# One visit instead of two: where a row tile's attention logits are multiplied in the first propagation step

## The chip, the cores and the metric

The kernel runs on one core of one Trainium2 chip. A core has five engines with queues of their own that meet only through semaphores: TensorE (PE: matrix products and transposes; PEld is its weight load), VectorE (DVE), ScalarE (ACT), GpSimd (POOL) and SyncE (SP, which here only issues DMAs). The metric is the device time of one execution in microseconds (us). Before the change the median of three runs is 1532.81 us (1531.89 to 1533.17).

## The reference, cut to what matters

Two graph layers follow one another on 2708 nodes with 256 features. The change lies in the first of them. It takes two propagation steps; each multiplies by a row-normalised adjacency matrix R, and by an attention matrix A that is computed anew in each step:

```
q = X @ W1.T @ W2.T                        # N x 64
k = X @ W3.T                               # N x 64
logits = q @ k.T                           # N x N
probs = softmax(logits)                    # per row
keep the largest of a row until their sum reaches 0.9, drop the rest, renormalise -> A
Xf = R @ Xf ;  Xa = A @ Xa ;  Z = Z + Xf @ U1[n].T + Xa @ U2[n].T
```

The second layer is a four-headed graph attention, and is not touched.

## The kernel before

**Tiles.** The 2708 rows are cut into 22 row tiles, sixteen of 128 rows and six of 110 (`rows`). For transposing, the tiles go in six groups (`groups`): four of four 128-row tiles, one of four 110-row tiles, one of two.

**What a row tile of step 0 needs.** `scores` (line 780) multiplies a row tile's q with all k. The contraction is 64 long, so the 2708 columns are held as two halves of 1354, one on partitions 0 to 63 and one on 64 to 127, and the two halves of a piece go through the two halves of the PE array. A half is cut into `pieces` of 512, 512 and 330 columns. For each piece the two products go into the two PSUM banks of a tile `lg`, and one ACT instruction takes the exponential of both banks into the row's `e` and sums it into a column of `zp`. POOL adds the three sums to `z` and makes `tau`, 0.9 of it. DVE then finds the row's threshold (`candidates`, `settle`, lines 888 and 899) and writes the kept values over `e` (line 965). After that PE transposes `e` group by group into `tr`, ACT copies each group to `eT`, and PE multiplies it with the features into the accumulator `att` (`turned` and `weigh`, lines 261 and 274); `e` has three buffers, so a tile is searched about three tiles ahead of its use.

**PSUM.** Its eight banks are all given out (line 564): four to `lg` (two buffers of two banks), one each to `walk0` and `walk1`, one to `att`, one to `tr`. In step 0 `free_bank` (line 650) hands out `walk0` and `walk1` in turn to the projections that follow a finished tile: the transposes of `xa` (line 774), a product with the next step's q and k weights for every second tile (line 761), and the term products (line 1252).

**The order.** TensorE, ScalarE, VectorE and GpSimd carry out the order in which the program writes their instructions. `step` (line 1307) takes the tiles in turn, and for each the six groups: first the *next* group's transposes and copy, then this group's products, then a *slot* (line 1292). A slot advances each running search by one stage, may begin a new search, advances the pieces that follow a finished tile, and then one stage of the mixing of adjacency blocks on POOL. Counting slots from 0, the search of tile t + 3 begins in slot 4 of tile t, and its stages stand so: slot 4, logits and exponentials of two pieces; slot 5, the third piece and the sums; slots 0 and 1 of the next tile, the maxima of the candidates; slot 2, the threshold; slot 3, the kept values. Tiles 0, 1 and 2 are searched ahead of the loop, beside the first projections (`terms1`, line 1231); the third of these searches is only half through when the loop begins. The last three tiles of step 0 begin no search.

**A tile boundary on PE.** After the last whole group of tile t PE carries out, in this order: the transposes of the first group of tile t + 1, the two products of tile t's last group, the third logit piece (slot 5), the transposes of the second group of tile t + 1, and the first products of tile t + 1. These last write `att`, which has one buffer: they wait until ACT has read tile t's sum out of it (`xa`, line 1325).

**DMAs.** SP's order is not written out by hand: a scheduler places the DMAs. SP stores the first terms (`c1`, line 1245) from the staging tile `cs`, which has two buffers, and loads the adjacency blocks that POOL mixes (`fetch`, line 677); before the first mixing POOL clears a column of each new block (line 702), and the load waits for that.

Of the kernel before, what the change touches and what calls it, by code (L numbers as in the profile page):

```python
# [8 lines left out]
F32 = mybir.dt.float32  # L9
BF16 = mybir.dt.bfloat16  # L10
I32 = mybir.dt.int32
AF = mybir.ActivationFunctionType
# [4 lines left out]
P = 128  # L17
# [28 lines left out]
def kernel(  # L46
# [16 lines left out]
    nc = tc.nc  # L63
    N, D = x.shape
    DA = w1T.shape[1]
    STEPS = u1T.shape[0]
    H, _, FO = gat_w.shape
# [8 lines left out]
    groups = []  # L76
# [8 lines left out]
    small = ctx.enter_context(tc.tile_pool(name="small", bufs=4))  # L85
# [122 lines left out]
    def share(g, tr):  # L208

        span, m = spans[g], rows[spans[g][0]]  # L210
        k = len(span) * H
        nc.tensor.transpose(
            tr[:k, 0, :m],
            s_src[:m, span[0] : span[-1] + 1, :].rearrange("p t h -> p (t h)"), ident[:m, :m],
        )
        nc.scalar.activation(line[:k, :m], tr[:k, 0, :m], AF.Exp, scale=1.0 - NEG_SLOPE)
        nc.sync.dma_start(shared[g], line[:k, :m])

    def spread(g, r):

        lines = shared[g].rearrange("(t h) m -> h t m", h=H)
        n = len(spans[g]) * rows[spans[g][0]]
        for k in range(2):
            for h in range(2):
                nc.sync.dma_start(
                    r[k][:, h, :n].rearrange("p (t m) -> p t m", t=len(spans[g])),
                    lines[2 * k + h].partition_broadcast(P),
                )
# [25 lines left out]
    def room(pool):  # L254

        return [
            pool.tile([P, N], F32, name="e")[:, : 2 * GW].rearrange("p (h i) -> p h i", h=2)
            for _ in range(2)
        ]
# [292 lines left out]
    def fast_layer0(ep, adjp):  # L552
# [69 lines left out]
        qT = keep.tile([P, N], F32, name="qT")  # L622
# [8 lines left out]
        kT = [wk.tile([P, HN], F32, name="junk"), keep.tile([P, HN], F32, name="kT1")]  # L631
# [15 lines left out]
        walking = []  # L647
        turns_taken = [0]

        def free_bank():  # L650

            if walking:
                return ps_lg.tile([P, 2, CHUNK], F32, name="lg")[:, 0].rearrange(
                    "p (a b) -> p a b", a=4
                )
            turns_taken[0] ^= 1
            return ps_wk.tile([P, CHUNK], F32, name=f"walk{turns_taken[0]}").rearrange(
                "p (a b) -> p a b", a=4
            )
# [120 lines left out]
        def scores(s, t):  # L780

            m = rows[t]
            cols = slice(off[t], off[t + 1])
            e = ep.tile([P, N], F32, name="e")
            halves = e.rearrange("p (h n) -> p h n", h=2)
            zp = small.tile([P, 3], F32, name="zp")
            for n, (c0, w) in enumerate(pieces):
                lg = ps_lg.tile([P, 2, CHUNK], F32, name="lg")
                for h in range(2):
                    part = slice(h * DA, (h + 1) * DA)  # L790
                    nc.tensor.matmul(  # L791
                        lg[:m, h, :w], qT[part, cols], kT[s][part, c0 : c0 + w],
                        start=True, stop=True,
                    )
                nc.scalar.activation(  # L795
                    halves[:m, :, c0 : c0 + w], lg[:m, :, :w], AF.Exp,
                    accum_out=zp[:m, n : n + 1],
                )
                if n == 1:
                    yield  # L800
            z = facts[s][0][:m, t : t + 1]
            nc.gpsimd.tensor_add(z, zp[:m, 0:1], zp[:m, 1:2])
            nc.gpsimd.tensor_add(z, z, zp[:m, 2:3])
            tau = new("tau", m)
            nc.gpsimd.tensor_scalar(tau, z, TOP_P, None, op0=ALU.mult)
            return e, z, tau

        def new(name, m):
            return small.tile([P, 1], F32, name=name)[:m]
# [161 lines left out]
        def search(s, t):  # L971

            e, z, tau = yield from scores(s, t)
            if s:
                seen = yield from survey(t, e, z, tau)
                src, rest = bound(t, e, z, tau, *seen)
            else:
                src, rest = e, tau
            yield
            cand = yield from candidates(s, t, src)  # L980
            yield
            ready[t] = e, (yield from settle(s, t, e, cand, rest))
# [231 lines left out]
        def after_attention0(t, xa):  # L1214

            m = rows[t]
            yield
            if t % 2 == 0:
                pair[:] = [rowp.tile([P, DC, 2 * P], F32, name="xT2", bufs=1)]
            both = pair[0]  # L1220
            xT = both[:, :, m * (t % 2) : m * (t % 2 + 1)]
            tp = free_bank()
            turn(xa, m, tp, nc.scalar.copy, xT)
            yield
            if t % 2:
                pj = free_bank().rearrange("p a b -> p (a b)")
                project(1, off[t - 1], 2 * m, pj, both, nc.scalar.copy, nc.scalar.copy)
                yield
            terms2(t, xT)
# [52 lines left out]
        early, walked, blending, begun, rows_kept = [], [], [], [], []  # L1282
# [4 lines left out]
        def advance(parts):  # L1287
            for g in list(parts):
                if next(g, parts) is parts:
                    parts.remove(g)  # L1290

        def slot(spend, begin=None):

            advance(going)
            if begin and begin[1] < NT:
                going.append(search(*begin))
                next(going[-1])
            advance(doing)
            if begun:
                next(mixing, None)  # L1300
            owed[0] += spend
            while owed[0] > 0:
                owed[0] -= 1
                if next(stream, True):
                    break

        def step(s, cur, spend):
            turned_first = None
            for t in range(NT):
                m = rows[t]  # L1310
                e, rden = ready[t]
                ac = ps_at.tile([P, CHUNK], F32, name="att")
                if s == 0 and t == NT - 1:
                    list(mixing)
                if s and t == NT - 2:
                    share(0, free_bank())
                if s and t == NT - 1:
                    ahead.extend(room(ep))
                    spread(0, ahead)

                def between(n):
                    last = n == len(groups) - 1
                    if last:
                        xa = heldp.tile([P, D], F32, name="xa1")
                        nc.scalar.activation(xa[:m], ac[:m, :D], AF.Copy, scale=rden)  # L1325
                        if s and t in c3:
                            nc.scalar.dma_start(c3[t][:m], xa[:m])
                            stored.add(t)
                        elif s:
                            held[t] = xa  # L1330
                        else:
                            doing.append(after_attention0(t, xa))
                    if (s, t) == (0, NT - 1):
                        for name, at in (("T3", 1), ("T2", 2), ("T1", 2), ("T4", 4)):
                            if n == at:
                                for part in J_PARTS:
                                    blend(name, *part)
                        if last:
                            next(stream)
                    slot(spend[n], (s, t + 3) if n == len(groups) - 2 else None)  # L1340

                def turn_next(n):
                    u = t + n // len(groups)
                    if u == NT:
                        return None
                    return turned(ready[u][0], rows[u], n % len(groups), tpp, ps_tr, nc.scalar.copy)

                turned_first = weigh(
                    ac[:m, :D], turned_first or turn_next(0), m,
                    lambda j: cur[: rows[j], j, 0:D], turn_next, between,  # L1350
                )
                ready.pop(t)
# [43 lines left out]
        with tc.manual_schedule(engines=engines):  # L1396
            query_weights()
            ahead = turn_x(groups[0])
            for n in range(len(groups)):
                c0, w = ahead  # L1400
# [430 lines left out]
```

## Time and profile before

| | |
|---|---|
| median of three runs | 1532.81 us |
| the profiled execution's own time | 1534.79 us |
| its span | 1532.7 us |
| granted TensorE clock over the span | 0.995 |
| busy share of the span: PE, DVE, ACT, POOL | 97%, 83%, 53%, 39% |
| step 0's attention loop | about 72 to 442 us |
| from tile to tile in it, first `att` product to first `att` product | 16.8 us, and 17.7 us in the tiles that also project q and k (128 rows) |
| step 0 loop from 72 to 397 us: PE, DVE, ACT, POOL busy | 323.6, 288.5, 141.9, 193.5 of 325 us |

The span is what the profiler recorded from the first instruction to the last; the execution's own time adds what lies around it. "Busy" counts the time in which an engine has an instruction in work. A busy PE is not yet a PE at its peak, since matmuls are pipelined and their ends are modelled: distances from start to start tell more than durations. In the timeline a row gives start, length, engine, line, operation, tiles, shape and how many instructions were merged (xN); a 32-bit product or transpose stands as one or more passes, and the count is that of passes. Bracketed is the idle time before the row and what ended it.

### The profile page before, as it was taken

To read this page: it belongs to the slowest core of one execution; us is meant where nothing else is said; L and a number is where in the kernel's file an instruction comes from. 1 tells how busy PE (TensorE), PEld (TensorE's weight loads), DVE (VectorE), ACT (ScalarE), POOL (GpSimd) and SP (SyncE) were. 2 spreads that over 40 slices of the span, in tenths; PEclk is the share of its full clock that TensorE was granted. 3 is DMA by queue.
4 is the path that set the end of the run, shared out by engine and by line. 5 is a ranking of instruction groups with operands and counts; after the bars stand their busy time and mean duration, and the time that the engine had idled before them with its cause. 6 is when DMAs were issued, how large, how long until landed. Compare 5 with 4: busy or idle time off the path is not lost. (4 is left out here: it accounts for less than half of the span.)

```text
span 1532.7 us, 29967 instructions
## 1 busy us (share of the span) xinstructions
PE 1492.8 (97%) x10537; PEld 1064.6 (69%) x10537; DVE 1277.1 (83%) x3749; ACT 804.9 (53%) x1495; POOL 594.5 (39%) x959
## 2 busy tenths in 40 slices
PE   8999999999999999999999999999999999999996
PEld 4477777776778889988988888887898223433343
DVE  3699888999714978888889898989895998999996
ACT  3444444444326556655655666666653344456474
POOL 0046657566013323323454554544444310035143
PEclk9999999999999999999999999999999999999998
DMA  6288888878037755554564555555455355334331
GB/s 166 66 246 277 247 247 281 266 234 255 12 102 235 211 165 167 161 162 137 159 199 142 165 183 170 182 166 178 137 151 178 109 172 167 100 104 135 88 105 53
DMA packets 214488, 255.97 MB, mean 167 GB/s; under 512 B 42145, under 2 KB 180541, under 8 KB 214329
## 3 DMA queue, kind: packets, MB, share of 16 engines
q1 hardware_dynamic: 205622, 246.62, 53.7%
q10 hardware_dynamic: 8707, 7.35, 1.5%
q8 instruction: 85, 1.39, 0.4%
q14 instruction: 74, 0.61, 0.1%
HBM read 190.10 MB, written 62.44 MB: 165 GB/s over the span
## 5 line engine op out<-in xcount | busy, mean ns | idle before, releaser
L816 ACT ACTIVATE junk<-e,minus,rth 128x2708 bf16<-128x2708 f32 (+1 forms) x88 | 232.9, 2646 | 52.5 <-POOL rth L848 51.7
L271 ACT COPY eT<-tr 128x512 f32<-128x512 f32 (+5 forms) x264 | 141.5, 536 | 199.0 <-PE tr L266 196.5
L284 PE MATMUL att<-xm,eT 128*128 128x256 f32 (+3 forms) x968 | 230.8, 379 | 0.3 <-ACT xa L1325 0.3
L284 PE MATMUL att<-ba,eT 128*128 128x256 f32 (+3 forms) x968 | 230.9, 379 | 0.0
L1618 PE MATMUL acc<-pt,v 128*32 128x512 f32 (+3 forms) x2112 | 222.9, 543 | 2.1 <-DVE pt L1606 1.1
L1606 DVE SCALAR_TENSOR_TENSOR pt<-e,tj,blk 128x1024 f32<-128x1024 f32 (+3 forms) x176 | 186.6, 1125 | 8.3 <-ACT xw L1265 5.4
L284 PEld LDWEIGHTS att<-xm,eT 128*128 128x128 f32 (+3 forms) x968 | 169.6, 186 | 22.0 <-ACT xa L1325 0.7
L284 PEld LDWEIGHTS att<-ba,eT 128*128 128x128 f32 (+3 forms) x968 | 169.5, 186 | 22.0 <-ACT eT L271 0.8
L795 ACT ACTIVATE e<-lg 128x1024 f32<-128x1024 f32 (+1 forms) x132 | 121.0, 921 | 105.7 <-PE lg L791 102.2
L1109 PE MATMUL walk<-xe,blk 128*128 128x128 f32 (+3 forms) x1386 | 172.9, 275 | 1.2 <-ACT xw L1123 0.7
L1109 PEld LDWEIGHTS walk<-xe,blk 128*128 128x128 f32 (+1 forms) x1386 | 164.4, 187 | 11.4 <-issue 7.4
L1618 PEld LDWEIGHTS acc<-pt,v 128*32 128x32 f32 (+1 forms) x2112 | 73.4, 109 | 130.8 <-issue 76.2
L266 PE MATMUL tr<-ident,e 128*128 128x128 f32 (+3 forms) x968 | 147.5, 271 | 4.8 <-ACT eT L271 4.8
L266 PEld LDWEIGHTS tr<-ident,e 128*128 128x128 f32 (+3 forms) x968 | 111.3, 139 | 47.1 <-issue 26.7
L1109 PE MATMUL walk<-xm,blk 128*128 128x128 f32 (+3 forms) x1034 | 131.3, 277 | 5.4 <-DVE u_sb L1119 2.9
L1109 PEld LDWEIGHTS walk<-xm,blk 128*128 128x128 f32 (+3 forms) x1034 | 124.2, 188 | 14.0 <-issue 6.1
L1628 PE MATMUL acc<-pt,sb 128*32 128x512 f32 (+3 forms) x1056 | 115.7, 542 | 0.0
L1606 DVE SCALAR_TENSOR_TENSOR pt<-r,tj,blk 128x1024 f32<-128x1024 f32 (+1 forms) x88 | 109.9, 1312 | 1.3 <-issue 0.6
L247 ACT ACTIVATE blk<-blk 128x1024 f32<-128x1024 f32 (+3 forms) x66 | 63.3, 960 | 82.5 <-DMA blk<-in_adjT_dram 76.2
L896 DVE MAX8 cand<-e 128x8 f32<-128x170 f32 (+1 forms) x352 | 85.9, 320 | 21.1 <-ACT e L795 21.0
L896 DVE MAX8 cand<-scr 128x8 f32<-128x97 f32 (+1 forms) x616 | 102.8, 244 | 0.0
L914 DVE MAX8 top<-work 128x8 f32<-128x128 f32 (+3 forms) x242 | 82.3, 340 | 8.3
(283 smaller groups left out, 2410.2 us busy)
## 6 DMA issues: line engine op xcount, KB each, us to landing
blk<-in_adjT_dram SPq DMA_DIRECT2D x68, 512.0 KB
blk<-S SPq DMA_DIRECT2D x48, 512.0 KB
blk<-D SPq DMA_DIRECT2D x24, 512.0 KB
blk<-in_adjT_dram SPq DMA_DIRECT2D x26, 440.0 KB
D<-blk SPq DMA_DIRECT2D x16, 512.0 KB
S<-scr SPq DMA_DIRECT2D x16, 512.0 KB
S<-blk SPq DMA_DIRECT2D x16, 512.0 KB
xm<-S SPq DMA_DIRECT2D x16, 512.0 KB
```

The lines of the kernel that those rows point to most:

```text
L247: nc.scalar.activation(bar, bar, AF.Sign)
L266: nc.tensor.transpose(tr[: rows[t], q, :m], e[:m, off[t] : off[t + 1]], ident[:m, :m])
L271: copy(eT[:k, : len(grp), :m], tr[:k, : len(grp), :m])
L284: nc.tensor.matmul(acc, eT[: rows[t], q, :m], value(t), start=(t == 0), stop=(t == NT - 1),)
L795: nc.scalar.activation(halves[:m, :, c0 : c0 + w], lg[:m, :, :w], AF.Exp, accum_out=zp[:m, n : n + 1],)
L816: nc.scalar.activation(junk[:m], e[:m], func, scale=rth, bias=minus1[:m], accum_out=acc)
L896: nc.vector.max(cand[:, n, :], src[:m, n * size : min(N, (n + 1) * size)])
L914: nc.vector.max(top[:, k : k + 8], work if k else flat)
L1109: nc.tensor.matmul(ac, blk[:k, j, :], MOVING[name](j, k, w), start=start and j == 0, stop=j == PAIRS - 1, skip_group_check=True,)
L1606: nc.vector.scalar_tensor_tensor(pt[:k, :gw], targets[g][h // 2][:k, h % 2, :gw], tj[:k, j, h : h + 1], bar, op0=ALU.max, op1=ALU.mult,)
L1618: nc.tensor.matmul(acc[h // 2][c][to : to + SIDE, :w], v[j][:k, h, o : o + SIDE], probs[n][h][:k, c0 : c0 + w], **at,)
L1628: nc.tensor.matmul(acc[2][c][h * SIDE : (h + 1) * SIDE, :w], sb[:k, j, h : h + 1].to_broadcast([k, SIDE]), probs[n][h][:k, c0 : c0 + w], **at,
```

## The change

In step 0's loop all logits of a row tile are multiplied in one visit, in slot 3 instead of in slots 4 and 5. The first two pieces go into `lg` as before; the third piece's two products go into two banks from `free_bank` (`walk0` and `walk1`) and are followed by a pause of one slot. In the next slot ACT takes their exponentials, now one instruction for each bank, with a sum for each, so `zp` has four columns and POOL adds once more. The test `one_visit` is true once the loop has begun (`begun`) and until the walks of the other matrix have (`walking`), so step 1 keeps the two visits and its slot: `len(groups) - 3 + s` is 3 in step 0 and 4 in step 1. (`begun and not walking` is the list `begun` itself while that is still empty, and the list is filled later: the search that is half through when the loop begins therefore pauses after its second piece as before, and sends its third piece by the new way.)

```diff
-            zp = small.tile([P, 3], F32, name="zp")
+            zp = small.tile([P, 4], F32, name="zp")
+            one_visit = begun and not walking
+
+            def logits(home, h, c0, w):
+                part = slice(h * DA, (h + 1) * DA)
+                nc.tensor.matmul(
+                    home, qT[part, cols], kT[s][part, c0 : c0 + w], start=True, stop=True
+                )
+
             for n, (c0, w) in enumerate(pieces):
+                if one_visit and n == 2:
+                    homes = [free_bank().rearrange("p a b -> p (a b)")[:m, :w] for _ in range(2)]
+                    for h, home in enumerate(homes):
+                        logits(home, h, c0, w)
+                    yield
+                    for h, home in enumerate(homes):
+                        nc.scalar.activation(
+                            halves[:m, h, c0 : c0 + w], home, AF.Exp,
+                            accum_out=zp[:m, n + h : n + h + 1],
+                        )
+                    continue
                 lg = ps_lg.tile([P, 2, CHUNK], F32, name="lg")
                 for h in range(2):
-                    part = slice(h * DA, (h + 1) * DA)
-                    nc.tensor.matmul(
-                        lg[:m, h, :w], qT[part, cols], kT[s][part, c0 : c0 + w],
-                        start=True, stop=True,
-                    )
+                    logits(lg[:m, h, :w], h, c0, w)
                 nc.scalar.activation(
                     halves[:m, :, c0 : c0 + w], lg[:m, :, :w], AF.Exp,
                     accum_out=zp[:m, n : n + 1],
                 )
-                if n == 1:
+                if n == 1 and not one_visit:
                     yield
             z = facts[s][0][:m, t : t + 1]
             nc.gpsimd.tensor_add(z, zp[:m, 0:1], zp[:m, 1:2])
             nc.gpsimd.tensor_add(z, z, zp[:m, 2:3])
+            if one_visit:
+                nc.gpsimd.tensor_add(z, z, zp[:m, 3:4])
...
-                    slot(spend[n], (s, t + 3) if n == len(groups) - 2 else None)
+                    slot(spend[n], (s, t + 3) if n == len(groups) - 3 + s else None)
```

## The prediction

> **What bounds the kernel now.** I read the busy totals first, then the stretches of step 0's loop, then who waits for whom in it, and last PE's timeline across two tile boundaries, one with logits and one without. The busy totals of the page and the stretch from 180 to 220 us (columns: PE, PEld, DVE, ACT, POOL busy, the granted clock, the DMA share, GB/s):
>
> ```profile
> PE 1492.8 (97%) x10537; PEld 1064.6 (69%) x10537; DVE 1277.1 (83%) x3749; ACT 804.9 (53%) x1495; POOL 594.5 (39%) x959
> ...
> 180.00:220.00 40.00, 40.00 (x199) 29.38 (x198) 33.91 (x87) 17.53 (x40) 27.74 (x30) 1.00 0.80 250
> ```
>
> PE has no free moment there at the full clock, and the waits of the loop hold no PE wait for DVE at all: a row's kept values are written 5.3 to 27 us before PE transposes them (end of the line-965 instruction to the first transpose of that tile, tile by tile). So PE alone sets the loop's length, and only PE's own work and gaps count. A boundary with logits (tile 8 to 9, 128 rows), from PE's timeline:
>
> ```profile
> 221.31 1.89 PE L284 MATMUL att<-xm,eT 110*128 110x256 f32 x8
> 223.14 1.99 PE L791 MATMUL lg<-junk,qT 64*128 64x512 f32 x8
> 225.06 0.66 PE L266 MATMUL tr<-ident,e 128*128 128x128 f32 x4
> 225.55 1.03 PE L284 MATMUL att<-xm,eT 110*128 110x256 f32 x4
> 226.51 0.83 PE L791 MATMUL lg<-junk,qT 64*128 64x330 f32 x4
> 227.26 0.66 PE L266 MATMUL tr<-ident,e 128*128 128x128 f32 x4
> 227.76 1.89 PE L284 MATMUL att<-xm,eT 128*128 128x256 f32 x8
> 229.49 0.38 PE L774 MATMUL walk<-ident,xa 128*128 128x128 f32 x2
> ```
>
> Read distances between starts. Undisturbed, eight att passes take 227.76 to 229.49, 1.73 us; ahead of logits they take 1.83. Four take 0.86 by half of that; ahead of the third piece they take 0.96. So entering a logit visit costs 0.10. Line 1252's four passes of 512 columns take 1.72 (231.87 to 233.59 in the same timeline), 0.43 each; eight logit passes take 1.92, so two go at a time, four steps of 0.43 and 0.20 on top. The third piece's 0.75 is likewise two steps of 0.43 x 330/512 = 0.28, and 0.20 on top. The four transposes after a visit take 0.50, against 0.44 after undisturbed work (229.70 to 230.14): 0.06. A visit therefore costs 0.36 us beyond its passes, and there are two for a tile.
>
> A boundary without logits (tile 19 to 20; those tiles begin no search), PE's timeline and then ACT's:
>
> ```profile
> 411.70 0.54 PE L266 MATMUL tr<-ident,e 110*128 110x110 f32 x4
> 412.08 1.03 PE L284 MATMUL att<-xm,eT 110*110 110x256 f32 x4
> 412.94 0.56 PE L266 MATMUL tr<-ident,e 110*128 110x110 f32 x4
> 413.67 1.98 PE L284 MATMUL att<-xm,eT 128*110 128x256 f32 x8 [0.16 <-ACT xa L1325]
> 415.49 0.35 PE L774 MATMUL walk<-ident,xa 110*128 110x110 f32 x2
> ```
>
> ```profile
> 413.15 0.47 ACT L1325 ACTIVATE xa<-att,rden 110x256 f32<-110x256 f32 x1 [0.28 <-PE att L284]
> ```
>
> Here PE does stall. The old tile's last products start at 412.08, ACT can read their sum at 413.15 and is done at 413.62, and the new tile's first products, which need the single att buffer, start at 413.67. With logits, that read (226.84 to 227.34) hid behind the third piece.
>
> **What the skill says.** *TensorEngine Tiling (Array Packing)*, Key Properties: changing the tiling mode drains TensorE, and tiles of one mode run in parallel. The trace agrees with both: 0.36 us around each 64-row visit, two passes at a time inside. *Perfetto Trace Analysis*, Optimization Strategy: a gap that repeats on the engine that should be saturated can mean that there is too little SBUF or PSUM for the next tile; the att wait of the tile boundary is that, and the trace shows it where no logits lie in between. *DMA: Bandwidth & Descriptors*, Queues, rings and completion order: each DMA engine consumes one issuer's descriptors in ring order, so a small store behind a large load waits for it; the trace of before has no such pair closely enough to price it.
>
> **The change part by part.**
>
> *The second visit goes.* At each boundary PE loses 0.10 + 0.75 + 0.06 = 0.91 us. The third piece then costs two more steps in the first visit, 0.55. Gain 0.36 for a tile, in 19 tiles (0 to 18): **-6.8 us**. The visit moves from slot 4 to slot 3; entering and leaving stay what they were.
>
> *The boundary is bared.* Without the third piece the wait for att shows. From the start of the old tile's last products it is 1.07 until ACT may read, 0.47 to read, 0.05 to PE: 1.59 us. PE's own work in between is 0.86 and the transposes, 0.44 for 128 rows, 0.37 for 110: a gap of 0.29 or 0.36. The eight att passes after the gap take 1.82 (413.67 to 415.49) against 1.73: 0.09 more. So 0.38 or 0.45; the 110-row boundary measures 3.79 from 411.70 to 415.49 against 0.38 + 0.86 + 0.38 + 1.73 = 3.35, which is 0.44. Fifteen boundaries lead into 128-row tiles, four into 110-row ones: 15 x 0.38 + 4 x 0.44 = **+7.5 us**. Bounds: -2 us if ACT reads att 0.1 sooner in every tile, +2 if later.
>
> *ACT.* The exponential of 660 columns (0.72) becomes two of 330. By the slope of the two sizes shown, (1.02 - 0.72) / 364 = 0.82 ns a column, each takes 0.45, plus its read of the sum: 0.35 us more for a tile on an engine that is busy 17.5 of 40. Would it make eT late? Count from the visit's first pass. The exponentials of the first two pieces end at 3.23 (223.14 to 226.37), then eT of the last group to about 3.5, then the two small ones to 4.4. PE leaves the visit at 2.47, then two transposes and eight att passes, and begins the next tile's transposes at 4.47; ACT can take those at about 5.2. Nothing is late; 0.7 us of cover. The copy that PE needs before those transposes, eT of the last group, is there 0.8 us early. I take **0**; without that cover at most 0.35 x 19 = 6.6.
>
> *The bank of the second small product* carries, in every other tile, a wait for its last reader, the copies of line 1257, which ended over 2 us before. Pairs of passes whose second product waited for a DMA long done stay paired in the trace of before. **0**; if pairs broke there, two steps of 0.28 in about ten tiles, +5.
>
> *DVE and POOL.* DVE's instructions keep their order and come one slot (some 2.5 us) sooner; one add more for a tile on POOL (0.19) is off PE's path with 5 us and more to spare. The half-done search of tile 2 comes one slot later, with 15 us to spare. **0**.
>
> *SP.* The diff does not show this. The scheduler now places the first adjacency loads among the c1 stores of the projections ahead of the loop, and POOL clears their columns at about 53 us instead of 78 us, since tile 2's sums are no longer ahead of that. In the kernel before they stood apart (SP's timeline):
>
> ```profile
> 40.01 32.92 SPq L1245 DMA_DIRECT2D c<-cs  x17
> 78.14 5.58 SPq L677 DMA_DIRECT2D blk<-in_adjT_dram  x6
> ```
>
> What stands behind them on SP are the c1 stores, and for those wait ACT's copies to cs (two buffers), and PE for a free walk bank. The first 512 KB load took 4.2 us from issue to its user (78.14 to 82.36). ACT idles 1.07 us before each of those copies and PE's second bank gives about 1 more, so a store may be 2 us late for nothing. Two stores stand directly behind 512 KB or more. I take 0.3 us each, **+0.6**; bounds 0 and +4 (both fully late, 4.2 - 2, on PE). The loads' early arrival gains nothing: POOL's waits for them lie off PE's path.
>
> Sum: -6.8 + 7.5 + 0.6 = **+1.3 us**. Everything after the loop keeps its order and shifts. Against the profiled span this gives 1532.7 + 1.3 = 1534.0; the median of the runs before, 1532.81, stands within 0.1 of that span (the profiled execution's own time, 1534.79, is 2.1 above it), so I predict 1534.1 for the runs.
>
> **The rivals.** *Faster:* the bared wait doesn't come, because something else still stands between old and new att, or ACT reads at once. Then the switches are clear gain, 1532.8 - 6.8 = 1526.0, or about 1529 with half the wait. For it: the diff cuts a cost that is real and on PE. Against it: PE's order at the boundary of the changed program is exactly that of tiles 19 and 20, where the wait stands twice in the trace. *Slower:* stores behind the early loads stall the projections ahead of the loop, at 53 to 70 us. It decides from a store that lands more than 2 us later than now; four stores so, at 1 us each, give 1532.8 + 0.7 + 4 = 1537.5. For it: PE is the bound there too. Against it: only some stores are behind large loads. A broken pairing in the walk banks would give a similar 1538. *The change doesn't do what it says:* the search under way at the loop's start goes half the old way; it is one of 20 and moves nothing.
>
> **How the numbers follow.** About 0.2% (3.1 us) is what a measurement of this kernel can tell from no change. The cancelling pair: 0.66, within about -2 to +4 and nearly all of it within 3.1. Wait absent or halved, faster: 0.15, between 1526 and 1529.7. Stalled stores or broken pairs, slower: 0.19, 1536 to 1541. Hence faster 0.16, same 0.62, slower 0.22. The range, 1529.3 to 1538.5, leaves about one in ten out on each side; the likeliest case's own is 1531 to 1536.8.
>
> **What would show it.** Right: one logit visit a tile of about 2.47 us to the next transposes; between tiles a gap of about 0.3 ahead of att, put down to xa, 19 times more than before; the loop's length unchanged within 2 us; adjacency loads from about 53 us. Wrong: no gap ahead of att; pairs of 330-column passes 0.28 or more apart; a copy to cs that waits for a DMA between 53 and 72 us; or an eT that PE waits for after the visit.

## The result, and the profile after

The changed kernel takes **1557.12 us** (median of six runs, 1555.33 to 1558.03); the kernel before took 1532.99 beside it (six runs, 1531.85 to 1534.41). The ratio is 1.0149, with a 95% interval of 1.0137 to 1.0161: 1.5% slower, where +1.3 us was forecast. It lies well outside the forecast range. The profiled execution of after has a span of 1556.1 us, its own time is 1558.03.

First where the 23.5 us of span lie. I cut both spans at three events: PE's first logit product, PE's first transposes of step 0's loop, and ACT's reading of the loop's last sum (`xa`). The 26.1 us ahead of the first logits are the same in both.

| | first logits to loop | the loop | after the loop | span |
|---|---|---|---|---|
| before | 45.91 | 369.37 | 1091.27 | 1532.7 |
| after | 47.62 | 389.42 | 1093.03 | 1556.1 |

The loop carries 20.05 of it. A tile takes 17.87 us instead of 16.82, and 18.73 instead of 17.69 where q and k are projected: 1.05 more, in 19 tiles. One line of the page shows where PE waits. The page of after, busy totals and costliest groups (the last columns are busy time, mean ns of one, and the idle time ahead of the group with what ended most of it):

```profile
PE 1497.3 (96%) x10537; PEld 1065.7 (68%) x10537; DVE 1282.7 (82%) x3749; ACT 809.2 (52%) x1535; POOL 598.8 (38%) x979
...
L266 PE MATMUL tr<-ident,e 128*128 128x128 f32 (+3 forms) x968 | 148.8, 272 | 20.1 <-ACT eT L271 20.1
```

The same group in the page of before:

```profile
L266 PE MATMUL tr<-ident,e 128*128 128x128 f32 (+3 forms) x968 | 147.5, 271 | 4.8 <-ACT eT L271 4.8
```

PE stands 15.3 us longer ahead of transposes, waiting for an `eT` copy. Starts, used below, tell more than this idle time, since the ends of matmuls are modelled. In the stretch from 180 to 220 us PE is no longer busy throughout (columns as in the prediction: PE, PEld, DVE, ACT, POOL busy, clock, DMA share, GB/s):

```profile
180.00:220.00 40.00, 37.50 (x187) 26.97 (x185) 34.24 (x90) 18.89 (x47) 28.12 (x32) 1.00 0.77 241
```

The boundary from tile 8 to 9 in after, PE's timeline:

```profile
231.23 1.99 PE L791 MATMUL lg<-junk,qT 64*128 64x512 f32 x8
233.05 0.72 PE L791 MATMUL walk<-junk,qT 64*128 64x330 f32 x4
233.70 0.43 PE L266 MATMUL tr<-ident,e 128*110 128x128 f32 x2
233.97 1.89 PE L284 MATMUL att<-xm,eT 110*128 110x256 f32 x8
236.65 0.66 PE L266 MATMUL tr<-ident,e 128*128 128x128 f32 x4 [0.79 <-ACT eT L271]
237.15 1.03 PE L284 MATMUL att<-xm,eT 110*128 110x256 f32 x4
238.04 0.66 PE L266 MATMUL tr<-ident,e 128*128 128x128 f32 x4
238.74 1.99 PE L284 MATMUL att<-xm,eT 128*128 128x256 f32 x8
```

The visit is there as described: 2.47 us from its first pass to the next transposes (231.23 to 233.70), the figure forecast. The transposes at 236.65 come 2.68 after the eight att passes began, where 1.73 is due: a stall of 0.95. And ACT over the same time:

```profile
229.70 0.60 ACT L271 COPY eT<-tr 110x512 f32<-110x512 f32 x1
234.22 1.03 ACT L810 ACTIVATE e<-lg 128x1024 f32<-128x1024 f32 x1 [3.91 <-POOL blk L716]
...
235.23 1.02 ACT L810 ACTIVATE e<-lg 128x1024 f32<-128x1024 f32 x1
...
236.23 0.37 ACT L271 COPY eT<-tr 110x256 f32<-110x256 f32 x1
```

ACT does nothing from 230.3 to 234.2, although its first logits were ready far sooner. In before the first exponential starts 1.22 us after the visit's first pass (223.14):

```profile
224.36 1.02 ACT L795 ACTIVATE e<-lg 128x1024 f32<-128x1024 f32 x1 [2.42 <-DVE work L916]
```

Here it is 2.99 (231.23 to 234.22). It starts 0.1 us after the two transposes of the old tile's *last group* (233.70) are done, and so it is in all 19 tiles of the loop: 2.94 to 2.99 us after the visit's first pass, and 0.04 to 0.09 us after the end of these two transposes. The copy of that group, `eT` at 236.23, stands behind both large exponentials on ACT; it reads the single `tr` bank, and PE needs that bank for the next tile. The bracket names POOL as the releaser, but the instruction waits for several engines, and the POOL instruction named (it starts at 230.57 and takes 3.24) had ended 0.4 us before. The waits of the loop, 60 to 470 us (total, times, longest), name PE's transposes eight times:

```profile
ACT e L810 <- PE tr L266: 31.7, 8, 4.0
```

The reason lies in the three `e` buffers. Tile t + 3's row takes the buffer of tile t, and the first write to it waits for all readers of the old row, here even for one that the program writes after it. In slot 4 tile t's last group has been turned already. In slot 3 its transposes are still to come: the program writes them after the visit, PE carries them out behind it, and the first exponential, which is written ahead of them, waits for them all the same. The columns don't even overlap: the last group turns columns 2488 to 2707, the first two pieces write 0 to 1023 and 1354 to 2377. The wait is for the tile, not for its columns.

That is a reading. Two things are to be tested: that it is the slot, and not the one visit, that costs the 20 us; and that it is the late exponential ahead of the copy, and not ACT's added instruction, that makes the copy late. A rival is that the visit's 2.47 us in one piece, or the four exponentials behind one another, are too much wherever they stand.

### The profile page after: what moved, and what is told of

It is laid out like the page before. It is cut to its first block, busy times and chain, and to the rows that moved or that the text cites. A ratio compares the mean times of both kernels' runs of the same rounds, so it can differ in the third digit from the quotient of the medians.

```text
span 1556.1 us, 30041 instructions
## 1 busy us (share of the span) xinstructions
PE 1497.3 (96%) x10537; PEld 1065.7 (68%) x10537; DVE 1282.7 (82%) x3749; ACT 809.2 (52%) x1535; POOL 598.8 (38%) x979
## 5 line engine op out<-in xcount | busy, mean ns | idle before, releaser
L810 ACT ACTIVATE e<-lg 128x1024 f32<-128x1024 f32 (+3 forms) x112 | 106.7, 958 | 131.2 <-PE lg L791 56.2
```

The lines of the kernel that those rows point to most:

```text
L810: nc.scalar.activation(halves[:m, :, c0 : c0 + w], lg[:m, :, :w], AF.Exp, accum_out=zp[:m, n : n + 1],)
```

## The experiments

**1. The early adjacency loads.** The search that is under way at the loop's start goes all the old way again; nothing else changes.

```diff
-            one_visit = begun and not walking
+            one_visit = bool(begun) and not walking
```

> The changed kernel, but the test for one visit is the truth value of the list, so the search that is under way when the loop begins keeps its old way and the adjacency loads stand behind all c1 stores again. If the 1.7 us by which the loop starts later (first transposes at 73.70 against 72.01 us) come from stores behind the early loads, the loop starts at 72.0 again and the time is 1555.4 us, 1.7 below the changed kernel. If the late start has another cause, 1557 stays.

Measured: 1555.63 us (four runs, 1551.4 to 1557.47), 1.0138 [1.0116, 1.016] of before (1533.35 there, fourteen runs). In its trace the stretch from the first logits to the loop is 45.91 again, as in before, and the loop 389.35, as in after. Of the kernels below, the two that keep the early loads have 47.59 and 47.52 there, and all the others 45.91. In after, SP's timeline ahead of the loop and then PE's showed this, among the stores of `cs` the loads of blocks, the first of them issued at 53.27:

```profile
58.33 0.32 SPq L1262 DMA_DIRECT2D c<-cs  x1
58.70 0.87 SPq L677 DMA_DIRECT2D blk<-in_adjT_dram  x2
59.66 2.15 SPq L1262 DMA_DIRECT2D c<-cs  x2
```

```profile
50.91 7.13 PE L1253 MATMUL walk<-u_sb,ba 128*128 128x512 f32 x16
58.63 5.42 PE L1253 MATMUL walk<-u_sb,ba 128*128 128x512 f32 x12 [0.58 <-ACT xe L1259]
...
64.65 1.97 PE L1253 MATMUL walk<-u_sb,ba 128*110 128x512 f32 x4 [0.60 <-ACT xe L1259]
```

and in this run PE runs through:

```profile
50.00 14.00 PE L1253 MATMUL walk<-u_sb,ba 128*128 128x512 f32 x32
```

At 0.43 us a pass the 16 passes that start at 50.91 in after are due to end at 57.79, and the next start at 58.63, 0.84 late; those at 64.65 are 0.86 late. So the loads among the `c1` stores cost 1.7 us of span, between the prediction's bounds, and nothing of the loop. The medians agree in size (1557.12 and 1555.63), but by themselves can't settle 1.5 us.

**2. One visit, in slot 4.** The visit stays whole, and only goes back to the slot where the search began before.

```diff
-                    slot(spend[n], (s, t + 3) if n == len(groups) - 3 + s else None)
+                    slot(spend[n], (s, t + 3) if n == len(groups) - 2 else None)
```

> The changed kernel with the search begun in slot 4, as before the change; still one visit and two walk banks. Theory A (in slot 3 the first exponential waits for the transposes of the old tile's last group, because the new row takes over that tile's buffer): in slot 4 these transposes are done, the first exponential starts 1.2 us after the visit's first pass, and what is left is the prediction's own sum, 1532.9 - 6.8 + 7.5 + 1.7 = 1535.3 us. Rival B (the two small exponentials and their extra sum make ACT late): they then stand directly ahead of nothing else and the time stays near 1550 or above. Rival C (the bared wait for att is dearer than reckoned): still about 1557.

Measured: 1537.54 us (ten runs, 1533.82 to 1541.02), 1.0025 [1.0012, 1.0038]. The loop is 370.42. Of the loop's 20 us 19 are gone with the slot alone. The time is 2.2 us above the 1535.3 expected.

The same with the loads late, as in experiment 1 (both edits):

> Begun in slot 4, one visit, and the list's truth value, so that neither the wait in slot 3 nor the early adjacency loads are left. Theory A: only the two terms are left that the prediction worked out and that cancel, -6.8 and +7.5; the last run's loop was 0.7 us longer than before from the first tile's sum to the twentieth's. Expected 1533.7 us against 1533.0 of before, a ratio of 1.0005. If something else in the change costs time, 1536 or more.

Measured: 1536.43 us (fourteen runs, 1535.23 to 1538.37), 1.0021 [1.0013, 1.0029] of before (1533.43 there, twenty runs). The loop is again 370.42. Its PE timeline at a boundary, and then ACT's first exponential:

```profile
239.57 1.99 PE L791 MATMUL lg<-junk,qT 64*128 64x512 f32 x8
241.39 0.72 PE L791 MATMUL walk<-junk,qT 64*128 64x330 f32 x4
242.04 0.66 PE L266 MATMUL tr<-ident,e 128*128 128x128 f32 x4
242.53 1.03 PE L284 MATMUL att<-xm,eT 110*128 110x256 f32 x4
243.47 0.66 PE L266 MATMUL tr<-ident,e 128*128 128x128 f32 x4
```

```profile
240.82 1.03 ACT L810 ACTIVATE e<-lg 128x1024 f32<-128x1024 f32 x1 [2.45 <-PE lg L791]
```

The exponential now starts 1.25 after the visit's first pass, and its releaser is the logits. The cancelling pair of the prediction stands here alone: the switch saved, the boundary bared. From the first tile's `xa` to the twentieth's the trace has 325.06 us against 324.40 before, +0.66, where the prediction's -6.8 + 7.5 gives +0.7. The medians say +3.0, of which the span of the profiled execution shows 1.2 (1533.9 to 1532.7). About 2 us of the medians I can't place. Scatter alone doesn't explain them, since the interval leaves out the ratio of 1.0005 that was expected, and the expectation had named 1536 or more as the sign that something else in the change costs time. The mean granted clock doesn't either: executions at 0.996 average 1536.0 us here and 1533.9 in before, those at 0.995 1536.6 and 1533.4. What it is stays open.

This run shows one thing more: a copy behind two large exponentials that start in time is hardly late. ACT's row after the second large exponential is

```profile
242.83 0.59 ACT L271 COPY eT<-tr 128x512 f32<-128x512 f32 x1
```

and PE's transposes behind it start 0.94 after 242.53, where 0.86 is due.

**3. Two visits, in slot 3.** The kernel before, its search begun one slot sooner. If the slot is the cause, the stall must show here too, without the one visit.

```diff
-                    slot(spend[n], (s, t + 3) if n == len(groups) - 2 else None)
+                    slot(spend[n], (s, t + 3) if n == len(groups) - 3 + s else None)
```

> The kernel before, with nothing but the search begun in slot 3 instead of 4; two visits as ever. Theory A: the first exponential waits for the last group's transposes here too, and starts about 2.4 us after the visit's first pass; but the third piece now stands in slot 4, ahead of the next tile's transposes, and covers nearly all of the lateness (eT of the last group done at 4.8, PE there at 4.8). The att wait of 0.38 is bared as well, since no piece is left at the boundary. Together 0.5 us a tile, 9 us, 1542. If the slot alone made the damage of the changed kernel, 1553 or more; if the slot doesn't matter, 1533.

Measured: 1543.84 us (five runs, 1541.96 to 1546.52), 1.007 [1.0057, 1.0084]; the loop 378.86, +9.5, which is 0.5 a tile. PE's timeline and ACT's at a boundary:

```profile
225.23 1.99 PE L791 MATMUL lg<-junk,qT 64*128 64x512 f32 x8
227.15 0.43 PE L266 MATMUL tr<-ident,e 128*110 128x128 f32 x2
...
229.24 0.83 PE L791 MATMUL lg<-junk,qT 64*128 64x330 f32 x4
230.10 0.66 PE L266 MATMUL tr<-ident,e 128*128 128x128 f32 x4
```

```profile
227.67 1.02 ACT L795 ACTIVATE e<-lg 128x1024 f32<-128x1024 f32 x1 [3.36 <-POOL blk L716]
...
229.68 0.37 ACT L271 COPY eT<-tr 110x256 f32<-110x256 f32 x1
```

The exponential starts 2.44 after the visit's first pass, and once more 0.1 after the last group's transposes; the shorter visit lets them through 0.55 sooner than in after. Over the 19 tiles it is 2.38 to 2.44, and 0.04 to 0.09. The copy still ends late, at 230.05, and PE's transposes begin just then. But the third piece, 0.83 us of logits, stands in between and hides nearly all of it: from 229.24 to 230.10 are 0.86, 0.11 more than the 0.75 before. The rest of the 0.5 is the att wait, which is bare here too. So the late exponential comes with slot 3, with or without the one visit; joining the visits both delays it further and takes the cover away.

**4. The exponentials behind the copy.** The changed kernel with late loads, and the exponentials of the first two pieces issued in slot 4, ahead of the two small ones. The last group's copy then has nothing in front of it.

```diff
+            waiting = []
...
                     yield
+                    for at, c1, lg in waiting:
+                        nc.scalar.activation(...)
...
+                if one_visit:
+                    waiting.append((n, c0, lg))
+                    continue
```

> Products in slot 3 as changed, but all four exponentials of a row in slot 4, behind the copy of the last group's eT, and the list's truth value. The wait for the transposes then costs nothing where it stands. Theory A with ACT's load: the four run from 3.4 to 6.4 us after the visit's first pass, and now the next tile's first eT is late; PE would want it at 5.8 and gets it at 7.0, a stall of 1.2, under which the att wait of 0.38 disappears. 0.85 us a tile more than slot4, 1550. If only the place of the wait counted, 1534; if ACT's order is without effect, 1555.

Measured: 1547.46 us (four runs, 1545.88 to 1550.89), 1.01 [1.0085, 1.0116]; the loop 382.94, +13.6 where some 17 were expected. PE's timeline, then ACT's:

```profile
231.40 1.03 PE L284 MATMUL att<-xm,eT 110*128 110x256 f32 x4
233.26 0.66 PE L266 MATMUL tr<-ident,e 128*128 128x128 f32 x4 [0.83 <-ACT eT L271]
```

```profile
229.49 0.37 ACT L271 COPY eT<-tr 110x256 f32<-110x256 f32 x1 [3.92 <-PE tr L266]
229.75 1.03 ACT L803 ACTIVATE e<-lg 128x1024 f32<-128x1024 f32 x1
...
232.59 0.61 ACT L271 COPY eT<-tr 128x512 f32<-128x512 f32 x1
```

The last group's copy is in time at 229.49, and the stall ahead of the next tile's first transposes is gone. Now the next copy, that of the next tile's first group (232.59), stands behind all four exponentials, and PE stalls 1.0 one group later (1.86 from 231.40 to 233.26, where 0.86 is due). The bank `tr` is the neck: here ACT has no room for some three microseconds of exponentials in one go between two groups of transposes.

**5. The last group turned early.** The changed kernel, with the last group's transposes and copy written ahead of the visit instead of behind it. This is the direct test: it takes away what the exponential waits for, and leaves slot 3. The copy moves with the transposes, ahead of the exponentials on ACT.

```diff
-            eT, ahead = ahead, turn_next(n + 1)
+            eT, ahead = ahead, held_turn.pop() if held_turn else turn_next(n + 1)
...
+            if early and n == len(groups) - 3:
+                held_turn.append(turn_next(n + 2))
             if between:
```

> The changed kernel with the visit still in slot 3, but the transposes of the tile's last group and their copy are written ahead of slot 3 instead of behind it. Theory A: the exponentials no longer wait for anything but their own products, and PE loses only the bared att wait: 1535 us, 22 below the changed kernel, with the first exponential 1.2 us after the visit's first pass instead of 3.0. Rival B (ACT has too much to do there) and rival C (att wait): no change, 1556 to 1558.

Measured: 1542.08 us (four runs: 1536.03, 1540.09, 1544.08, 1546.4), 1.0064 [1.0042, 1.0086]; the loop of the profiled execution, the fastest of them, is 371.26. PE's timeline, then ACT's:

```profile
239.01 0.38 PE L266 MATMUL tr<-ident,e 128*110 128x128 f32 x2
239.32 1.99 PE L794 MATMUL lg<-junk,qT 64*128 64x512 f32 x8
241.14 0.72 PE L794 MATMUL walk<-junk,qT 64*128 64x330 f32 x4
241.79 1.99 PE L285 MATMUL att<-xm,eT 110*128 110x256 f32 x8
243.62 0.60 PE L266 MATMUL tr<-ident,e 128*128 128x128 f32 x4
```

```profile
240.57 1.02 ACT L813 ACTIVATE e<-lg 128x1024 f32<-128x1024 f32 x1 [0.72 <-PE lg L794]
```

The exponential starts 1.25 after the visit's first pass, in the same slot 3, with the same four exponentials; the stall is gone (241.79 to 243.62), and 18.2 of the loop's 20 us with it. So neither the length of the visit nor the longer work of ACT was at fault. That the copy no longer stands behind the exponentials is a second difference, which this run can't tell from the first; experiment 2 speaks against it as the cause, since there a copy behind two timely exponentials was 0.08 late at the boundary shown. The median is 7 us above the 1535 expected, and the four executions lie 10 us apart. The same with late loads:

> One visit in slot 3 with the last group's transposes written ahead of it, and the list's truth value. Theory A: the loop as in the run before, 1.5 us longer than that of the kernel before, and the loop starting at its old time: 1534.5 us, ratio 1.001. The last run's single times lay between 1536 and 1546 while its profiled loop was short; if these times belong to the order and not to the chip at that moment, they stay above 1538.

Measured: 1538.99 us (seven runs, 1536.08 to 1540.65), 1.0034 [1.0023, 1.0045]; the loop 373.33. One gap of 1.68 us near the loop's end (384.07) is a tile whose kept values DVE wrote just before; the rest of the distance to the 1534.5 expected, about 2.8 us, stays open, as in experiment 2. The median lies above 1538, the expectation's own mark, so some of it belongs to this order of instructions and not to the chip at the moment of the run before.

**6. One visit, in slot 5.** If slot 3 bares the att wait and slot 4 too, slot 5 stands between old and new `att`: the visit would hide ACT's read, and only the saved switch is left. With late loads; the small exponentials follow without a pause.

```diff
-                    yield
                     for h, home in enumerate(homes):
...
-                    slot(spend[n], (s, t + 3) if n == len(groups) - 3 + s else None)
+                    slot(spend[n], (s, t + 3) if n == len(groups) - 1 - s else None)
```

> One visit in slot 5, with its exponentials behind it without a pause, and the list's truth value as in boolbegun. The visit then stands between the old tile's last products and the new tile's second transposes, where the third piece stood before. Theory A with the prediction's prices: one visit's 0.36 us is saved in 19 tiles, the att wait is covered by the visit (ACT reads att while PE multiplies logits), the buffer is free: 1532.9 - 6.8 = 1526 us. If rival B holds, the exponentials make the second group's eT late and the time is 1533 or more. If the price of a visit was wrong, 1533.

Measured: 1528.07 us (five runs, 1526.89 to 1530.28), **0.9965 [0.9951, 0.9979]**: faster than both kernels. The loop is 364.20, -5.2; a tile takes 16.47 or 17.34 us, 0.35 less than before. PE's timeline, then ACT's:

```profile
237.01 1.99 PE L791 MATMUL lg<-junk,qT 64*128 64x512 f32 x8
238.83 0.72 PE L791 MATMUL walk<-junk,qT 64*128 64x330 f32 x4
239.48 0.66 PE L266 MATMUL tr<-ident,e 128*128 128x128 f32 x4
239.97 1.89 PE L284 MATMUL att<-xm,eT 128*128 128x256 f32 x8
```

```profile
237.12 0.47 ACT L1341 ACTIVATE xa<-att,rden 128x256 f32<-128x256 f32 x1 [0.23 <-PE att L284]
...
238.27 1.02 ACT L809 ACTIVATE e<-lg 128x1024 f32<-128x1024 f32 x1 [0.68 <-PE lg L791]
```

ACT reads `att` while PE is in the visit, and the products at 239.97 don't wait. Of the 6.8 forecast for the switch 5.2 arrive. Most of the rest is one gap, PE's timeline ahead of tile 15's first transposes, and what DVE did before it:

```profile
319.86 1.89 PE L284 MATMUL att<-xm,eT 110*128 110x256 f32 x8
322.86 0.63 PE L266 MATMUL tr<-ident,e 128*128 128x128 f32 x4 [1.11 <-DVE e L981]
```

```profile
314.01 4.86 DVE L938 CUSTOM_DVE_ANT_0 sums<-sums,top 128x56 f32<-128x56 f32 x1
...
319.11 3.60 DVE L981 SCALAR_TENSOR_TENSOR e<-e,fact 128x2708 f32<-128x2708 f32 x1
```

The search begins a slot later and has less slack. In this tile the kept values are done at about 322.7, and PE begins at 322.86, 1.27 late. In two more tiles PE comes only 0.15 and 0.32 us after them, where no tile of before has less than 5.3.

A fourth `e` buffer, which should take the wait away in slot 3, was not tried. A row takes 2708 x 4 bytes, 10.6 KB, of each partition; whether there is room for one more, no run shows.

## Why the prediction was wrong, point by point

**The step that failed is "ACT".** It let the exponentials start as soon as their products were there ("The exponentials of the first two pieces end at 3.23 (223.14 to 226.37), then eT of the last group to about 3.5 … The copy that PE needs before those transposes, eT of the last group, is there 0.8 us early") and took 0. That 3.23 was read off a visit in slot 4. In slot 3 the row's buffer is still being read: the exponentials ended at 5.02 after the visit's first pass (231.23 to 236.25), and the copy at 5.37, against the 4.47 at which PE wanted it. The term should have been 0.95, not 0, in each of 19 tiles. Experiment 5 took the wait away and left the slot and the one visit, and 18 us of the loop went with it (15 by the medians, 1557.12 to 1542.08). The question left out was one of the buffer: who is the last reader of the tile that this write replaces, and is that reader now ahead of it or behind? The profile of before shows where that reader stands: the last group's transposes are in PE's order ahead of the 221.31 row, so ahead of slot 4's logits but behind slot 3's place. That the write waits for a reader written after it, only the runs show.

In its closing list the prediction had named "an eT that PE waits for after the visit" as a sign of being wrong. That is what came, but none of its cases had it as a mechanism with a price, so the range didn't reach it. The bound that it gave, 0.35 x 19 = 6.6, covered ACT's added time only, and so was no bound.

**The other terms.** The loop's +1.05 a tile can be put together from starts in after's timeline. The stall is 0.95 (2.68 from the att passes to the transposes, where 1.73 is due), and the restart 0.06 and 0.04 (transposes 0.50 instead of 0.44, four att passes 0.90 instead of 0.86). The att gap is 0.26 (0.70 from transposes to att, where 0.44 is due), and the att passes after it take 0.10 more. Less the saved switch of 0.36, that is 1.05.

- *The second visit goes*: 0.36 a tile forecast; 0.35 measured where nothing covers it (experiment 6). *TensorEngine Tiling (Array Packing)*, Key Properties, of the Trainium skill says that changing the mode drains TensorE. 0.35 is the price of a whole visit here, entering, inside and leaving together; how much of it is the drain, no run shows.
- *The boundary is bared*: 0.38 forecast, 0.26 + 0.10 measured. In experiment 2 the pair comes to +0.66 from the first `xa` to the twentieth, where +0.7 was forecast; the medians there say +3.0, and about 2 us of that stay open.
- *The banks of the small products*: 0 forecast, and the pairs stay whole. The third piece takes 0.65 from 233.05 to the next transposes, two steps of 0.28 and the leaving.
- *SP*: +0.6 forecast, bounds 0 to +4; +1.7 measured in the trace (experiment 1). Right in kind and in the number of places, two; each cost 0.85 instead of 0.3.
- *After the loop*: nothing forecast, +1.8 in the trace. The same stretch is -2.0 to +2.1 in the other kernels, in no order that follows their edits; I read it as scatter of single executions, but no run isolates it.

**The rivals.** "Faster" is true of another slot: with the visit between old and new `att` the switch is a clear gain (experiment 6). It was rightly held unlikely for the diff as it stood. "Slower by stalled stores" happened in small. "The change doesn't do what it says" is out: there is one visit a tile.

## What to carry to other kernels

When an instruction that fills a rotating buffer is moved forward, look for the last reader of the tile that it replaces before counting anything else: the wait seen here is for the whole tile, even where the columns don't overlap and the reader is written later, and it falls on whatever is queued behind the writer on its engine. A duration from the trace holds for the place in which it was taken; here the same exponential started 1.2 us after its visit in one slot and 3.0 in the one before. And when a piece of work is cut out of a boundary, ask what else it was hiding: of the three slots tried, the best place for the joined visit was the one where a wait needed cover anyway.

## What the runs showed that was not expected

- A DVE instruction on 56 columns (line 922 of before, the custom operation of the threshold) takes 0.22 us in 11 of before's 22 tiles of step 0 and 0.80 to 5.56 in the others. In every tile in which it takes longer than 0.22, in before, in after and in experiment 6, tensor-tensor operations of POOL run beside it, and it ends 0.07 or 0.08 us after the end of one of them. The one at 206.41 in before (5.55 us) ends at 211.96; a row of POOL operations began at 205.03, and its sixth ended at 211.88. Where it takes 0.22, POOL carries out no such operation beside it, but for 0.15 us in one tile of experiment 6. No run varies this, and POOL's times in a profile are rough. In experiment 6 a long one (4.86 us) stands ahead of the kept values for which PE waited 1.27 us.
- A store of `c1` behind loads of 512 KB on SP's queue made PE 0.84 and 0.86 us late at two places ahead of the loop (1.7 us in all), by way of ACT, which waits 2.59 and 2.21 us for a store before its next copy to `cs`, where 1.07 is usual.
- The releaser that a bracket names can be none of the cause. The first exponential of after is put down to POOL's `blk`, in a tile where it began 0.1 us after PE's transposes. The fixed distance to those, in all 19 tiles of each kernel that takes the exponentials in slot 3 ahead of the last group's transposes, told more than the name.
